# The order of VectorE's work within a step: a group's results behind the norm, a joining group's sums behind the statistics

## The chip, the cores and the metric

The kernel runs on one core of a Trainium2 chip. The time is the device time of one launch in microseconds (us). Before the change the median of three runs is 4190.81 us (4182.11 to 4192.11).

The core has engines with an instruction queue each, which work side by side and wait for one another through semaphores: TensorE (PE in the profile; its weight loads are PEld) for matmuls and transposes, VectorE (DVE), ScalarE (ACT), GpSimd (POOL), and SyncE (SP), which issues DMAs. TensorE writes its results into PSUM, a small memory that VectorE and ScalarE read; everything else lies in SBUF.

## What is computed

12,500 nodes with 256 channels each go through one graph layer and then, each node for itself, through 30 iterations of a small network. All is fp32.

```python
xn = layernorm(x)
x = x + relu(segment_sum((xn @ W_gnn)[src] * edge_weight, dst)) + mix(xn)   # 200,000 edges

def step(h):                       # 30 times
    h = h + 0.01 * tanh(h)
    h = h * sigmoid(h)
    h = layernorm(h) * ln_w + ln_b
    return h @ W + b

x = x + step applied 30 times to layernorm(x)
```

`mix` is a linear attention over all nodes; what is left of it per node, once its key-value products are summed, is one 256 x 256 matrix. The gains and offsets of the layernorm are folded into the matrices beforehand.

## The kernel before

**Tiles and groups.** The nodes lie in 98 tiles of 128 rows, and four tiles make a group: 24 groups of 1024 columns per partition and one of 512. A first part (the first 470 us or so) normalises x, sums the key-value products and prepares the matrices. The rest, which the change is about, is a loop over 803 steps.

**Items and steps.** A planner, `plan`, gives each step `k` at most one item: `("mix", g)`, the product of group g with the matrix of mix; `("W", g)`, the product of its gathered and summed neighbours with the graph weight; or `("pass", g, it)`, one of the 30 iterations. There are 25, 23 and 750 of them. Up to five groups are between their first and last pass at the same time (`ABREAST`), and a group's passes are at least four steps apart (`APART`). The planner has its own costs in us for an item, a gather and so on; they decide only which item stands in which step. The instructions of each engine stand in the order in which the loop writes them: nothing is reordered later.

**An item takes three steps.** Its work is spread so that TensorE always has something that is ready:

- step k: for a pass, the transposes of the normalised group `z` into PSUM (`transposes`, line 1057), copied by ScalarE to `zT` (line 1064);
- step k + 1: the product, `matrix` (line 1070), sixteen matmul passes into the PSUM tile `po`. There are two `po` buffers, so the product of step k + 1 writes the buffer that the product of step k - 1 wrote and that step k reads;
- step k + 2: what is done with the product. For a pass, ScalarE's tanh (`act1`, line 1016), VectorE's sum h + 0.01 tanh(h) (`act2`, line 1022), which is the last reader of `po`, and ScalarE's SiLU (line 1023). After that `stats`: VectorE's statistics (`bn_stats`, line 1029), and GpSimd's variance plus epsilon (line 1033) and power -1/2 (`rs`, line 1035). For the last pass of a group, VectorE adds the product to `base`, the group's result (line 1129, two halves), and SP writes it out. For a mix item VectorE adds product and x (line 1135, and two more, line 1140, for the first two groups). For a W item it adds the product and the stored rows (line 1144) and then the ReLU of that to `base` (line 1145).

**The norm.** `normed` (line 1043) makes `z` from the statistics, four VectorE instructions for a full group. In step k it is called for the items of steps k + 1 and k + 2 whose statistics are there. A group whose passes are four steps apart has statistics in step k + 2, norm in k + 3 and transposes in k + 4.

**A joining group.** When a group leaves, the next one starts (`fresh`, with the step k3 in which it does). Its first layernorm and first tanh, sum and SiLU aren't a pass: statistics of `base` in k3 and k3 + 1 (lines 1195 to 1203), its normalised half in k3 + 2 and k3 + 3 (ScalarE line 1174, VectorE line 1178), its tanh at the end of k3 + 3 (line 1183, through `act1`), its sums and SiLU (`act2`, lines 1022 and 1023) in k3 + 4, its statistics at the end of k3 + 5. Its first pass can stand in k3 + 7 at the earliest. An output stands two steps after a group's last pass, which is k3 + 2 of the group that joins in its place.

**The order within a step, before.** VectorE's queue in step k has: the edge selections (lines 213 to 226), a clearing of PSUM (line 276), then the sum of the pass of step k - 2, or the output, mix or W work in its place; the joining group's sum, where k is k3 + 4; the norm; the joining group's normalised half; the statistics of the pass of step k - 2; the joining group's statistics.

Beside all this, GpSimd gathers the rows of the edges (line 187), and TensorE sums them in pieces in between (lines 239 and 261), up to about 3470 us.

Of the kernel before, what the change touches and what calls it, by code (L numbers as in the profile page):

```python
# [31 lines left out]
def gps_layer(  # L32
# [48 lines left out]
    def rows_io(ap, tl, t0, nt, load, eng):  # L81
        full = nt if (t0 + nt) * P <= N else nt - 1
        parts = []
        if full:
            parts.append((tl[:, :full, :], ap[t0 * P : (t0 + full) * P, :].rearrange("(g p) c -> p g c", p=P)))
        if full < nt:
            parts.append((tl[:TAIL, full, :], ap[(t0 + full) * P : N, :]))
        for s, d in parts:
            if load:
                eng.dma_start(out=s, in_=d)  # L90
            else:
                eng.dma_start(out=d, in_=s)
# [192 lines left out]
    class KeyValue:  # L285
# [19 lines left out]
        def normed(self):  # L305
            rs8 = kvw.tile([P, 2 * HEADS], F32, name="rs8")
            nc.vector.reciprocal(rs8, self.sd)
            nc.vector.tensor_tensor(
                kns[self.t % 3][:, :, :D], self.pkv, rs8[:, :, None].to_broadcast([P, 2 * HEADS, D]), ALU.mult
            )  # L310
# [315 lines left out]
    with tc.If(n_out > 0):  # L626
        with ExitStack() as pg_:
# [12 lines left out]
            for t in range(NE):  # L640
# [8 lines left out]
                d = gp.tile([P, 1], F32, name="d")  # L649
                nc.vector.tensor_copy(d[:rows], d_i[:rows])  # L650
                d = d[:rows]
# [354 lines left out]
    norm, zs, zTs, pos, xts, first_norm = {}, {}, {}, {}, {}, {}  # L1006
# [3 lines left out]
    def flat(h, nt):  # L1010
        return h[:, : nt // 2].rearrange("p q c j -> p (q c j)")
# [7 lines left out]
    def act2(gi, h, s):  # L1019
        nt = groups[gi][1]  # L1020
        sf = flat(s, nt)
        nc.vector.scalar_tensor_tensor(sf, sf, 0.01, flat(h, nt), op0=ALU.mult, op1=ALU.add)  # L1022
        nc.scalar.activation(sf, sf, AF.Silu)  # L1023

    def stats(gi, s):
        t0, nt = groups[gi]
        st = hp.tile([P, G // 2, 6], F32, name="st")
        for q in range(nt // 2):
            nc.vector.bn_stats(st[:, q, :], s[:, q].rearrange("p c j -> p (c j)"))  # L1029

        sv = st.rearrange("p q (j f) -> p (q j) f", f=3)
        ve = fp.tile([P, G], F32, name="ve")
        nc.gpsimd.tensor_scalar(ve[:, :nt], sv[:, :nt, 2], 1.0 / C, EPS, ALU.mult, ALU.add)  # L1033
        rs = hp.tile([P, G], F32, name="rs")
        nc.gpsimd.tensor_tensor(rs[:, :nt], ve[:, :nt], mhalf[:, :nt], ALU.pow)  # L1035
        norm[gi] = (s, sv, rs)
# [41 lines left out]
    item = lambda k: steps[k][0] if 0 <= k < K and steps[k][0] else (None, None)  # L1078
    quads_of = lambda k: steps[k][1] if k < K else 0
    fresh = []  # L1080
    written = {}
    selections(ed.summed + quads_of(0) - ed.selected)
    for k in range(K + 3):
# [33 lines left out]
        last = kind2 == "pass" and item(k - 2)[2] == FFN_ITERS - 1  # L1117
# [3 lines left out]
            copies(gi)  # L1121
        if kind2 == "pass" and not last:
            act2(g2, pos.pop((kind2, g2)), s2)
        elif last:
            t0, nt = groups[g2]
            for q in range(nt // 2):
                h = pos[kind2, g2][:, q].rearrange("p c j -> p j c")
                r = slice(2 * q, 2 * q + 2)
                nc.vector.tensor_tensor(base[g2][:, r, :], h, base[g2][:, r, :], ALU.add)  # L1129
            pos.pop((kind2, g2))  # L1130
            rows_io(out, base[g2], t0, nt, False, nc.sync)
            written[g2] = k
        elif kind2 == "mix":
            nt = groups[g2][1]
            nc.vector.tensor_tensor(base[g2], pos.pop((kind2, g2))[:, :nt, :], xts.pop((kind2, g2))[:, :nt, :], ALU.add)
            if g2 < ed.weighted:
                aT = ed.aT.pop(g2).rearrange("p k (g n) -> p k g n", n=P)
                for i in range(KC):
                    bk = base[g2][:, :, i * P : (i + 1) * P]
                    nc.vector.scalar_tensor_tensor(bk, aT[:, i], 0.0, bk, op0=ALU.max, op1=ALU.add)  # L1140
        elif kind2 == "W":
            nt = groups[g2][1]
            ac = xts.pop((kind2, g2))[:, :nt, :]
            nc.vector.tensor_tensor(ac, pos.pop((kind2, g2))[:, :nt, :], ac, ALU.add)
            nc.vector.scalar_tensor_tensor(base[g2], ac, 0.0, base[g2], op0=ALU.max, op1=ALU.add)

        for g3, k3 in fresh:
            if k == k3 + 4:  # L1150
                act2(g3, *first_norm[g3])
        for d in (1, 2):
            kind3, g3 = item(k + d)[:2]
            if kind3 == "pass" and g3 in norm:
                normed(g3)
        for g3, k3 in fresh:
            nt = groups[g3][1]
            if k in (k3 + 2, k3 + 3):
# [24 lines left out]
                    first_norm[g3] = (h, act1(g3, h))  # L1183
        if kind2 == "pass" and not last:
            stats(g2, s2)
        start = steps[k][2] if k < K else None
        if start is not None:
            fresh.append((start, k))
# [50 lines left out]
```

## Time and profile before

| | |
|---|---|
| median of 3 runs | 4190.81 us (4182.11 to 4192.11) |
| the profiled execution's own time | 4187.49 us |
| its span, first to last instruction | 4185.7 us |
| mean granted TensorE clock | 0.991 |
| VectorE busy | 3401.4 us (81%) |
| ScalarE busy | 2523.0 us (60%) |
| GpSimd busy | 2577.9 us (62%) |

One execution was profiled. The page of the profile gives the busy time of each engine, the chain of work that ended last (followed back from the last instruction, at each step to what released it), and the groups of instructions by source line with their counts and mean durations. Other views of the same trace give the waits (who waited for whom, how long in total, how often and the longest), and the timeline (start, duration, engine, line, operation, tiles written and read, shapes, count; in brackets the idle time of the engine just before, and what ended it). A tile name such as `po<-w,zT` says that `po` is written and `w` and `zT` are read. `x4` is a run of four instructions of a kind, merged.

Durations in the steps, from the groups with shapes kept apart: one sum of a pass (line 1022, 128 x 1024) 1.21 us, one norm instruction (line 1043, 128 x 256) 0.42 us, of which a full group has four that overlap a little, one statistics instruction (line 1029, 128 x 512) 0.68 us, two to a group; one half of an output (line 1129, 128 x 512) 0.68 us, the sum of a mix item (line 1135) 1.21 us, the two of a W item (lines 1144 and 1145) 1.22 and 1.23 us; ScalarE's SiLU (line 1023) 1.06 us.

### The profile page before, as it was taken

The numbers are of one execution on the slowest core, as the hardware profiler recorded it, in microseconds if no ns is written. First come the engines' busy times: TensorE is split into PE (matmuls) and PEld (weight loads), VectorE is DVE, ScalarE is ACT, GpSimd is POOL, SyncE is SP. The second block draws the span as 40 slices with busy tenths as digits, with TensorE's granted clock in tenths as the row PEclk, the third lists the DMA queues.
The fourth block names the chain that finished last, engine by engine and source line by source line (L and its number), as shares of the span: only waits on it lengthen the run. The fifth ranks groups of instructions, "written<-read, shape, count | busy, mean of one in ns | idle before, by whom it ended". The sixth has DMA issues, their size and how long they took to land.

```text
span 4185.7 us, 67249 instructions
## 1 busy us (share of the span) xinstructions
PE 4057.6 (97%) x23817; PEld 3358.3 (80%) x23817; DVE 3401.4 (81%) x7400; ACT 2523.0 (60%) x3762; POOL 2577.9 (62%) x3189
## 2 busy tenths in 40 slices
PE   8897899999999999999999999999999999999999
PEld 5444678888888888888888888888888888888888
DVE  8554568888888888888888888888888888888887
ACT  7331246666666666666666666666656666667775
POOL 3564666777777777777777777777667652222222
PEclk9898999999999999999999999999999999999999
DMA  8332532222222222222222222222222210000000
GB/s 262 108 87 72 147 98 66 65 61 65 75 61 72 76 64 74 73 66 71 72 65 72 77 65 72 70 74 61 72 70 59 65 50 14 6 6 1 1 1 23
DMA packets 147685, 278.31 MB, mean 66 GB/s; under 512 B 28048, under 2 KB 97198, under 8 KB 147342
## 3 DMA queue, kind: packets, MB, share of 16 engines
q0 software_dynamic: 75024, 204.97, 17.0%
q1 hardware_dynamic: 72173, 68.42, 5.4%
q8 instruction: 194, 3.18, 0.3%
q14 instruction: 150, 1.22, 0.1%
q10 hardware_dynamic: 144, 0.52, 0.0%
HBM read 247.68 MB, written 26.12 MB: 65 GB/s over the span
## 4 chain that ended last, share of the span: by engine, by line
PE 77%; DVE 11%; ACT 3%; issue 3%; POOL 2%; another core or an unknown queue 1%; POOLq 0%; DVEq 0%; ACTq 0%
PE po L1070 53%; PE pt L1057 13%; PE pq L239 4%; DVE z L1043 4%; PE pkv L290 3%; PE pa L261 3%; DVE st L1029 2%; DVE s L1022 2%; ACT s L1016 2%; POOL rs L1035 1%; PE pacc L316 1%; ACT s L1023 1%; POOL xg L187 0%; DVE big L1129 0%
## 5 line engine op out<-in xcount | busy, mean ns | idle before, releaser
L1070 PE MATMUL po<-w,zT 128*128 128x256 f32 x11760 | 2669.8, 380 | 4.8 <-ACT zT L1064 2.3
L1070 PEld LDWEIGHTS po<-w,zT 128*128 128x128 f32 x11760 | 2178.4, 190 | 285.2 <-issue 7.8
L187 POOL DMA_INDIRECT xg<-xnd,src_i x1563 | 1597.4, 1022 | 512.9 <-issue 308.6
L1023 ACT ACTIVATE s<-s 128x1024 f32<-128x1024 f32 (+1 forms) x750 | 780.5, 1041 | 598.5 <-DVE s L1022 584.9
L1043 DVE TENSOR_SCALAR z<-s,st,rs 128x256 f32<-128x256 f32 x2940 | 1031.5, 418 | 100.7 <-POOL rs L1035 96.0
L1029 DVE BATCH_NORM_STATS2 st<-s 128x6 f32<-128x512 f32 x1470 | 938.7, 680 | 181.6 <-ACT s L1023 163.8
L1022 DVE SCALAR_TENSOR_TENSOR s<-s,po 128x1024 f32<-128x1024 f32 x725 | 864.3, 1192 | 251.4 <-ACT s L1016 181.3
L1016 ACT ACTIVATE s<-po 128x1024 f32<-128x1024 f32 x725 | 729.6, 1006 | 209.0 <-PE po L1070 197.6
L1064 ACT ACTIVATE zT<-pt 128x512 f32<-128x512 f32 x1470 | 801.5, 602 | 61.2 <-PE pt L1057 55.0
L1057 PE MATMUL pt<-ident,z 128*128 128x128 f32 x5880 | 792.7, 276 | 38.9 <-DVE z L1043 37.5
L1057 PEld LDWEIGHTS pt<-ident,z 128*128 128x128 f32 x5880 | 670.1, 141 | 182.6 <-issue 81.6
L1035 POOL TENSOR_TENSOR rs<-ve,mhalf 128x4 f32<-128x4 f32 (+1 forms) x750 | 763.3, 1018 | 62.5
L1033 POOL TENSOR_SCALAR ve<-st 128x4 f32<-128x4 f32 (+1 forms) x750 | 147.3, 196 | 933.6 <-DVE st L1029 889.0
L250 ACT COPY sq<-pq 128x256 f32<-128x256 f32 x196 | 72.4, 369 | 284.3 <-PE pq L239 198.2
L239 PE MATMUL pq<-xg,sel 128*32 128x256 f32 x3126 | 222.9, 386 | 8.5 <-issue 6.4
L290 PE MATMUL pkv<-wkv,big 128*128 128x512 f32 x392 | 201.3, 634 | 9.3 <-DVEq L626 4.9
L239 PEld LDWEIGHTS pq<-xg,sel 128*32 128x32 f32 x3126 | 84.7, 109 | 112.1 <-issue 69.5
L261 PE MATMUL pa<-selq,sq 128*128 128x192 f32 (+1 forms) x784 | 163.4, 331 | 9.3 <-ACT sq L250 3.6
L275 ACT COPY aT<-pa 128x128 f32<-128x128 f32 x196 | 51.4, 262 | 194.1 <-PE pa L261 145.6
L261 PEld LDWEIGHTS pa<-selq,sq 128*128 128x128 f32 (+1 forms) x784 | 137.9, 192 | 22.0 <-ACT sq L250 4.7
L301 DVE TENSOR_REDUCE v<-sq 128x8 f32<-128x512 f32 x98 | 66.7, 680 | 92.4 <-ACT sq L297 78.4
L297 ACT ACTIVATE sq<-pkv 128x512 f32<-128x512 f32 x98 | 57.9, 591 | 115.3 <-PE pkv L290 69.1
(163 smaller groups left out, 1553.2 us busy)
## 6 DMA issues: line engine op xcount, KB each, us to landing
xg<-xnd,src_i POOLq DMA_INDIRECT x1563
xt<-in_x_dram SPq DMA_DIRECT2D x48, 512.0 KB
xnd<-xt SPq DMA_DIRECT2D x24, 512.0 KB
out_dram<-big SPq DMA_DIRECT2D x24, 512.0 KB
xt<-accw SPq DMA_DIRECT2D x22, 512.0 KB
ac<-accw SPq DMA_DIRECT2D x2, 512.0 KB
xg<-in_dst_dram SPq DMA_DIRECT2D x6, 128.0 KB
xg<-in_src_dram SPq DMA_DIRECT2D x6, 128.0 KB
```

The lines of the kernel that those rows point to most:

```text
L187: nc.gpsimd.indirect_dma_start(out=ed.xg[t], out_offset=None, in_=xnd, in_offset=bass.IndirectOffsetOnAxis(ap=src_i[:, t : t + 1], axis=0),)
L239: nc.tensor.matmul(ed.pq[j * 2 * WIN : (j + 1) * 2 * WIN, :], lhsT=sel[:, j, :], rhs=ed.xg.pop(q * Q + j), start=(q % 2 == 0), stop=last, ...
L261: nc.tensor.matmul(pa[:, k, :], lhsT=sq[:rows, k * P : (k + 1) * P], rhs=selq[:rows, :], start=False, stop=(o == NO - 1), skip_group_check ...
L1016: nc.scalar.activation(flat(s, nt), flat(h, nt), AF.Tanh)
L1022: nc.vector.scalar_tensor_tensor(sf, sf, 0.01, flat(h, nt), op0=ALU.mult, op1=ALU.add)
L1023: nc.scalar.activation(sf, sf, AF.Silu)
L1029: nc.vector.bn_stats(st[:, q, :], s[:, q].rearrange("p c j -> p (c j)"))
L1035: nc.gpsimd.tensor_tensor(rs[:, :nt], ve[:, :nt], mhalf[:, :nt], ALU.pow)
L1043: nc.vector.tensor_scalar(z[:, j, :], s[:, j // 2, :, j % 2], sv[:, j, 1:2], rs[:, j : j + 1], ALU.subtract, ALU.mult)
L1057: nc.tensor.transpose(pt[:, i, k, :], z[:, 2 * q + i, k * P : (k + 1) * P], ident)
L1064: nc.scalar.activation(zT[:, 2 * q : 2 * q + 2], pt, AF.Copy, bias=1.0)
L1070: nc.tensor.matmul(po[:, j // 2, :, j % 2] if paired else po[:, j, :], lhsT=lhsT(j, k), rhs=rhs[:, k, :], start=(k == 0 and (j % 2 == 0 or ...
```

## The change

Three pieces of the step's second half change places; no instruction is added or taken away. `act2` of a pass keeps its place. The norm comes directly behind it; then the outputs, mix and W work (an `elif` becomes an `if`, as the norm now stands between); then, as before, the joining group's normalised half and the statistics of the pass; and behind these the joining group's sum and SiLU, which stood ahead of the norm.

```diff
             copies(gi)
         if kind2 == "pass" and not last:
             act2(g2, pos.pop((kind2, g2)), s2)
-        elif last:
+
+
+
+        for d in (1, 2):
+            kind3, g3 = item(k + d)[:2]
+            if kind3 == "pass" and g3 in norm:
+                normed(g3)
+
+        if last:
             t0, nt = groups[g2]
             for q in range(nt // 2):
                 h = pos[kind2, g2][:, q].rearrange("p c j -> p j c")
...
             nc.vector.tensor_tensor(ac, pos.pop((kind2, g2))[:, :nt, :], ac, ALU.add)
             nc.vector.scalar_tensor_tensor(base[g2], ac, 0.0, base[g2], op0=ALU.max, op1=ALU.add)
-
-
-
-        for g3, k3 in fresh:
-            if k == k3 + 4:
-                act2(g3, *first_norm[g3])
-        for d in (1, 2):
-            kind3, g3 = item(k + d)[:2]
-            if kind3 == "pass" and g3 in norm:
-                normed(g3)
         for g3, k3 in fresh:
             nt = groups[g3][1]
             if k in (k3 + 2, k3 + 3):
...
         if kind2 == "pass" and not last:
             stats(g2, s2)
+        for g3, k3 in fresh:
+            if k == k3 + 4:
+                act2(g3, *first_norm[g3])
         start = steps[k][2] if k < K else None
         if start is not None:
             fresh.append((start, k))
```

## The prediction

> **What bounds the kernel now.** I read the page first. The chain that ended last is three quarters TensorE, and TensorE's engine row is busy for 97% of the span.
>
> ```profile
> PE 4057.6 (97%) x23817; PEld 3358.3 (80%) x23817; DVE 3401.4 (81%) x7400; ACT 2523.0 (60%) x3762; POOL 2577.9 (62%) x3189
> ...
> PE 77%; DVE 11%; ACT 3%; issue 3%; POOL 2%; another core or an unknown queue 1%; POOLq 0%; DVEq 0%; ACTq 0%
> ```
>
> So a step costs what TensorE needs for it: eight transposes 0.87 us and sixteen matmul passes 3.46 us, start to start, with now and then the edge sums between. Whatever the other engines do is free until TensorE waits for it, and what it waits for is in the table of its waits from 470 us on, where the scheduled steps run (total us, times, longest):
>
> ```profile
> PE pt L1057 <- DVE z L1043: 37.5, 41, 2.4
> PE po L1070 <- DVE s L1022: 2.5, 5, 1.5
> ...
> PE po L1070 <- DVE xt L1144: 1.1, 2, 0.5
> PE po L1070 <- DVE big L1135: 0.5, 2, 0.3
> PE po L1070 <- DVE big L1129: 0.3, 1, 0.3
> ```
>
> The first row is what an earlier norm can win, 37.5 us at the very most. The other rows matter as much: PSUM holds two step results (`po`), so the product of step k+1 overwrites the result that VectorE reads in step k. The last three rows are that wait for exactly the instructions now moved back; today it is rare.
>
> **First part: outputs, mix and W behind the norm.** Nothing is added or removed. In each of 56 steps a block (outputs 2 x 0.68 us, line 1129; mix 1.21, line 1135; W 1.22 + 1.23, lines 1144 and 1145) changes places with the norm, four instructions of 1.38 us together, 1.28 until what follows them starts. A step with W, in the timeline (start, length):
>
> ```profile
> 2951.77 1.22 DVE L1144 TENSOR_TENSOR xt<-po,xt 128x1024 f32<-128x1024 f32 x1
> 2953.02 1.23 DVE L1145 SCALAR_TENSOR_TENSOR big<-xt,big 128x1024 f32<-128x1024 f32 x1
> 2954.16 1.38 DVE L1043 TENSOR_SCALAR z<-s,st,rs 128x256 f32<-128x256 f32 x4
> ...
> 2952.64 1.04 PE L1057 MATMUL pt<-ident,z 128*128 128x128 f32 x8
> 2953.51 2.76 PE L1070 MATMUL po<-w,zT 128*128 128x256 f32 x12
> ```
>
> Today W's sum lets go of `po` at 2952.99 and the product starts at 2953.51, in time by 0.52. With the norm first (its `rs` is long there) the sum runs 2953.05 to 2954.27: TensorE waits 0.8. And what does the earlier norm win? The transposes that read it start at 2958.06, 3.9 us after its present start. Nothing. I read all 56 steps so: norm at the later of VectorE free and `rs` ready, then the sum, against the start of the next product. Late are 10 of 13 mixes (14.1 us), 12 of 22 W (11.2) and 11 of 21 outputs (14.1), 39.4 in all. Where `rs` isn't ready, VectorE now idles for it, which the sum used to cover; this makes the worst ones (2.1 to 2.6). Waits of 1.6 on products and of 3.0 on transposes stand in the same steps today and are in the 39.4: **+35**. Bounds: 0, if VectorE's queue stands emptier than I read, to +39. I take the reading, since the rows give the release to 0.05 us. The output's DMA from SP leaves 1 to 3 us later and is no one's wait except at the very end, where no norm stands before it.
>
> **Second part: the joining group's sums behind the statistics.** Its line 1022 (1.22 us) moves behind the norm (1.28) and the statistics (1.2), about 2.5 us later. ScalarE's order stays, so its SiLU of the joining group (1.06) comes 2.5 us later too, and queued behind it on ScalarE are the next step's tanh, its copies of zT and its SiLU. A join as it is:
>
> ```profile
> 3502.25 1.22 DVE L1022 SCALAR_TENSOR_TENSOR s<-s,po 128x1024 f32<-128x1024 f32 x1 [1.23 <-ACT s L1016]
> 3503.39 1.22 DVE L1022 SCALAR_TENSOR_TENSOR s<-s,big 128x1024 f32<-128x1024 f32 x1
> 3503.51 2.19 ACT L1023 ACTIVATE s<-s 128x1024 f32<-128x1024 f32 x2 [0.31 <-DVE s L1022]
> 3504.52 1.37 DVE L1043 TENSOR_SCALAR z<-s,st,rs 128x256 f32<-128x256 f32 x4
> 3505.08 1.31 PE L1057 MATMUL pt<-ident,z 128*128 128x128 f32 x8 [1.70 <-DVE z L1043]
> ...
> 3505.61 1.00 ACT L1016 ACTIVATE s<-po 128x1024 f32<-128x1024 f32 x1
> ...
> 3505.82 1.28 DVE L1029 BATCH_NORM_STATS2 st<-s 128x6 f32<-128x512 f32 x2
> ...
> 3507.01 1.20 DVE L1022 SCALAR_TENSOR_TENSOR s<-s,po 128x1024 f32<-128x1024 f32 x1
> ...
> 3508.50 1.38 DVE L1043 TENSOR_SCALAR z<-s,st,rs 128x256 f32<-128x256 f32 x4 [0.29 <-POOL rs L1035]
> ...
> 3509.68 1.04 PE L1057 MATMUL pt<-ident,z 128*128 128x128 f32 x8
> ```
>
> The gain: the norm starts at 3503.39, the transposes 0.56 behind it at 3503.95, and of the wait of 1.70 there go 1.13. The price: statistics 3504.69 to 3505.97, joining sums until 3507.10, its SiLU 3507.14 to 3508.20. The tanh, at 3505.61 today, starts at 3508.20 and ends at 3509.2. VectorE's next sums come at 3509.26, 2.25 late; the norm after them at 3510.40 rather than 3508.50; its transposes at 3510.96. TensorE would have been there at 3503.95 + 4.60 = 3508.55, so it waits 2.4, and stands 1.3 behind today's 3509.68. The joining group's own statistics and power on POOL, the last before its first pass, move by 1.9, and its first transposes from 3514.42 to 3516.3: 1.9 lost in this join.
>
> Carried on so through 23 joins (the first two have no other passes beside them): the waits of today that go are 11.8 us; 12 joins lose 1.6 to 1.9 net (21.6), 7 about 0.5 (3.5), four nothing, where a W or mix step leaves ScalarE free: **+25** net. Bounds: -12, if ScalarE's later start is caught up before a transpose, to +29, if no slack at POOL takes 0.29 off. I take +25, since in these steps VectorE's rows stand end to start and four groups in turn leave each norm only one step ahead.
>
> **What they share.** In 11 joins a late output holds TensorE for about 1.0 two steps before, while ScalarE's and VectorE's chain in the join hangs on the joining group's norm and tanh, not on TensorE. So the same us is not lost twice: -11. The mixes before 660 us meet waits on the norm that stand there already, 3 more: **-14** (bounds -25 and 0).
>
> **The clock.** In the steps there are two half-speed stretches of 3.4 us in the granted clock, at 2690 and at 3564, each just after TensorE waited 2.35 for a joining step's norm; sixteen passes then take 5.28 where 3.62 is usual, 1.7 lost. A third wait of 2.36 passed free, and so did one of 1.79. These two go (-3.4), and about two of the new waits of over 2 us should pay it again: 0, bounds -3.4 and +10 (six more).
> The Trainium skill (TensorE: Matmul & The Clock Gate, "HAM oscillation") has idle gaps above about 3.4 us as what throttles the array. By it no wait here, old or new, would cost clock, and these two stretches would not be there; the rows say otherwise, and I go by them.
>
> **Sum.** 35 + 25 - 14 + 0 = +46 us. On the profiled execution that is 4185.7 + 46 = 4231.7 of span, 4233.5 with the 1.8 around it; the median of the runs shown lies 3.3 above that execution: **4237 us**.
>
> **Rivals.** (1) *Only the results are late*: the joins come out even, ScalarE (60% busy) making good its 2.5 us; nothing is shared then except early on, and half of the lateness is absorbed by steps in which VectorE runs ahead: 35/2 to 35 - 3, 4208 to 4222. For: ScalarE waits 562 us for line 1022's sums in the steps. Against: just in the join it does not. (2) *The clock multiplies*: each of some 12 new waits near 2 us costs a half-speed stretch, 12 x 1.7 = 20, and one feeds the next: about 4262. For: 2 of 3 today. Against: waits of 1.7 to 1.8 went free. (3) *No difference*: all lands in slack, 4191. Against: TensorE has about 50 us of idle in 3,700 us of steps. (4) *Faster*: the norm is the one late thing in a joining step. With it ahead of the sums the 11.8 us go, also the 3.0 beside outputs and W, and 3.4 of clock, 18 in all: 4173. It decides if the wait for `po` and ScalarE's queue together cost under 18 us, a third of a us for each moved block. For: the 37.5 us are the largest wait there is. Against: the W step above, where the norm had 3.9 us to spare.
>
> **How the numbers follow.** Forecast 4237, own range 4222 to 4262, chance 0.60; rival 1 0.20; rival 2 0.08; rival 3 0.06; rival 4 0.06. The range 4205 to 4262 takes in the forecast's and rival 1's. What a measurement of this kernel can tell from no change is about 0.3%, 12.6 us: slower than 4203.4 is 0.88 (all of the first three but a little of rival 1), within 0.07, faster 0.05.
>
> **What would show it.** Right: TensorE's waits for lines 1129, 1135 and 1144 (by their new numbers) grow from 2 to some 30 us; waits on the norm fall in the joining step and rise in the two steps after; ScalarE waits over 2 us for the joining sums. Wrong: if the waits for `po` stay under 10 us, my release times are off; if the norm's wait falls well below 37.5 in total, the chain through ScalarE is off, and rival 4 is near.

## The result, and the profile after

The changed kernel takes 4240.94 us (median of four runs, 4235.25 to 4242.6) against 4187.83 us of the kernel before (median of four, the three shown above and one more, 4182.11 to 4192.11): 53.1 us more, a ratio of 1.0123 with a 95% interval of 1.0109 to 1.0137. The forecast was 4237, 46 us above the kernel before, with a range of 4222 to 4262.

The page of the changed kernel, engine rows and the chain that ended last:

```profile
PE 4066.9 (96%) x23817; PEld 3361.1 (79%) x23817; DVE 3404.7 (80%) x7400; ACT 2520.3 (59%) x3762; POOL 2599.7 (61%) x3189
...
PE 69%; DVE 16%; ACT 4%; issue 4%; POOL 3%; another core or an unknown queue 1%; DMA 0%; DVEq 0%; POOLq 0%; ACTq 0%
```

VectorE's busy time is what it was (3401.4 before), as nothing was added. But on the chain TensorE has 8% of the span less than before (69% for 77%), and VectorE has 5% more, ScalarE and GpSimd 1% each: TensorE now stands and waits. For whom, its waits in the steps tell (total us, times, longest); outputs, mix and W are lines 1137, 1143 and 1152 here:

```profile
PE pt L1057 <- DVE z L1043: 44.5, 42, 3.6
PE po L1070 <- DVE big L1137: 11.8, 10, 2.1
PE po L1070 <- DVE xt L1152: 9.7, 9, 1.9
PE po L1070 <- DVE big L1143: 9.2, 6, 2.0
PE po L1070 <- DVE s L1022: 4.1, 6, 1.5
```

The three rows for results that let go of `po` late come to 30.7 us in 25 waits, where they were 1.9 in five. The wait on the norm, which the change puts first, isn't less than before but more, 44.5 for 37.5. Half-speed stretches of 3.4 us are seven among the passes instead of two.

The W step that the prediction showed, now (start, length; in brackets the idle time before and what ended it):

```profile
2984.51 1.37 DVE L1043 TENSOR_SCALAR z<-s,st,rs 128x256 f32<-128x256 f32 x4
2985.37 1.04 PE L1057 MATMUL pt<-ident,z 128*128 128x128 f32 x8
2985.81 1.21 DVE L1152 TENSOR_TENSOR xt<-po,xt 128x1024 f32<-128x1024 f32 x1
2987.05 1.22 DVE L1153 SCALAR_TENSOR_TENSOR big<-xt,big 128x1024 f32<-128x1024 f32 x1
...
2987.07 3.29 PE L1070 MATMUL po<-w,zT 128*128 128x256 f32 x14 [0.67 <-DVE xt L1152]
```

From the transposes to the product it is 1.70 us rather than 0.87, so 0.83 are lost; 0.8 was worked out. The product starts 0.05 behind the end of W's sum, and the norm that W's sum had to let past is for transposes that start at 2991.73.

And the join that the prediction carried through, from the joining step on:

```profile
3549.80 1.38 DVE L1043 TENSOR_SCALAR z<-s,st,rs 128x256 f32<-128x256 f32 x4
...
3550.36 1.32 PE L1057 MATMUL pt<-ident,z 128*128 128x128 f32 x8
3551.10 1.28 DVE L1029 BATCH_NORM_STATS2 st<-s 128x6 f32<-128x512 f32 x2
...
3552.30 1.21 DVE L1022 SCALAR_TENSOR_TENSOR s<-s,big 128x1024 f32<-128x1024 f32 x1
...
3553.54 1.06 ACT L1023 ACTIVATE s<-s 128x1024 f32<-128x1024 f32 x1 [2.56 <-DVE s L1022]
3554.50 1.01 ACT L1016 ACTIVATE s<-po 128x1024 f32<-128x1024 f32 x1
...
3555.54 1.22 DVE L1022 SCALAR_TENSOR_TENSOR s<-s,po 128x1024 f32<-128x1024 f32 x1 [2.04 <-ACT s L1016]
3556.68 1.38 DVE L1043 TENSOR_SCALAR z<-s,st,rs 128x256 f32<-128x256 f32 x4
...
3557.23 1.32 PE L1057 MATMUL pt<-ident,z 128*128 128x128 f32 x8 [2.10 <-DVE z L1043]
```

The wait of 1.70 in front of the first transposes is gone. ScalarE, though, stands 2.56 us before the joining group's SiLU, the tanh of the next pass comes behind that, VectorE stands 2.04 us for the tanh, and TensorE 2.10 us for the norm one step later, where it didn't wait at all before.

### The profile page after: what moved, and what is told of

Its sections match the earlier page's. It is cut to its first block, busy times and chain, and to the rows that moved or that the text cites. A ratio compares the mean times of both kernels' runs of the same rounds, so it can differ in the third digit from the quotient of the medians.

```text
span 4240.8 us, 67172 instructions
## 1 busy us (share of the span) xinstructions
PE 4066.9 (96%) x23817; PEld 3361.1 (79%) x23817; DVE 3404.7 (80%) x7400; ACT 2520.3 (59%) x3762; POOL 2599.7 (61%) x3189
## 4 chain that ended last, share of the span: by engine, by line
PE 69%; DVE 16%; ACT 4%; issue 4%; POOL 3%; another core or an unknown queue 1%; DMA 0%; DVEq 0%; POOLq 0%; ACTq 0%
PE po L1070 48%; PE pt L1057 12%; DVE z L1043 6%; PE pq L239 4%; DVE st L1029 4%; DVE s L1022 3%; PE pa L261 2%; PE pkv L290 2%; ACT s L1016 2%; POOL rs L1035 2%; ACT s L1023 1%; PE pacc L316 1%; POOL xg L187 1%; DVE big L1137 0%
## 5 line engine op out<-in xcount | busy, mean ns | idle before, releaser
L1070 PE MATMUL po<-w,zT 128*128 128x256 f32 x11760 | 2678.7, 381 | 35.9 <-DVE big L1137 11.8
L1057 PE MATMUL pt<-ident,z 128*128 128x128 f32 x5880 | 794.7, 276 | 47.1 <-DVE z L1043 44.5
L1033 POOL TENSOR_SCALAR ve<-st 128x4 f32<-128x4 f32 (+1 forms) x750 | 168.0, 224 | 976.4 <-DVE st L1029 932.6
```

Of the source, the lines that this page charges most:

```text
L1057: nc.tensor.transpose(pt[:, i, k, :], z[:, 2 * q + i, k * P : (k + 1) * P], ident)
L1070: nc.tensor.matmul(po[:, j // 2, :, j % 2] if paired else po[:, j, :], lhsT=lhsT(j, k), rhs=rhs[:, k, :], start=(k == 0 and (j % 2 == 0 or ...
```

## The experiments

Each ratio is against the kernel before on the same chip. The chip that ran the first four took 4087.58 us for the kernel before, 100 us less than the others did; some 80 of these lie ahead of the first pass (its transposes begin at 391 us in `e1_results` and at 474 in the profile of the kernel before). So times of whole kernels are compared on the same chip only. The kernel before has one profile, from one of the slower chips; where a stretch of it is set beside one of the first four, the text says so. `e4_silu_late` is one of these four and takes nearly the time of the kernel before, so the others are set beside it too.

**One part alone.** `e1_results` leaves the joining sums where they stood and moves only the results behind the norm:

```diff
+        for g3, k3 in fresh:
+            if k == k3 + 4:
+                act2(g3, *first_norm[g3])
         for d in (1, 2):
...
             stats(g2, s2)
-        for g3, k3 in fresh:
-            if k == k3 + 4:
-                act2(g3, *first_norm[g3])
```

(a diff against the changed kernel, with lines left out at `...`). 

> Outputs, mix and W work behind the norm; the joining group's sums ahead of the norm as in the kernel before. Theory (PSUM is let go of late): TensorE's waits for the three lines that read po come to 28 to 32 us as in the changed kernel, waits on the norm stay at 34 to 38, two to four half-speed stretches in the steps: 4188 + 28 to 36 = 4216 to 4224 us. Rival (only the joining group's part costs): waits for po of a few us at most, 4183 to 4193.

Measured: 4115.31 for 4087.58, +27.7 us, ratio 1.0070 (1.0056 to 1.0084). TensorE's waits in the steps (outputs, mix and W are lines 1140, 1146 and 1155):

```profile
PE pt L1057 <- DVE z L1043: 18.1, 26, 1.8
PE po L1070 <- DVE big L1140: 11.5, 10, 2.1
PE po L1070 <- DVE big L1146: 11.3, 10, 2.0
PE po L1070 <- DVE xt L1155: 9.6, 9, 2.8
```

The waits for `po` are all there, 32.4 us, so this loss needs nothing of the other part. The time all but fits (28 to 36 expected), but the wait on the norm does not: 18.1 rather than 34 to 38. A late output holds TensorE back by 1 to 2 us just ahead of the joining step, whose norm then comes in time. So this part also takes some of the old waits off. Behind step 148, where the mix steps are nearly over, it needs 14.3 us more than the kernel before (3038.0 for 3023.7, each in its one profile, on two chips). From the first transposes of a pass to step 148 it needs 9.4 us more than `e4_silu_late` on the same chip (676.3 for 666.9).

`e2_joining` moves only the joining sums behind the statistics. 

> Only the joining group's sums moved behind the statistics; the results ahead of the norm as in the kernel before. Theory (ScalarE's queue stands behind the late SiLU): waits for po as in the kernel before, waits on the norm 55 to 65 us rather than 37.5 (12 gone in the joining steps, 35 new in the two steps behind them), 4188 + 20 to 29 = 4208 to 4217. Rival (it wins what the joining step's norm waited): 4170 to 4180.

Measured: 4121.31, +33.7 us, ratio 1.0086 (1.0072 to 1.0099); it was dearer than expected. Its waits:

```profile
PE pt L1057 <- DVE z L1043: 48.6, 44, 2.5
PE po L1070 <- DVE s L1022: 3.6, 7, 1.5
```

The waits on the norm are 48.6, less than the 55 to 65 expected, and half-speed stretches are four instead of two. From step 148 to the last pass this kernel needs 3046.0 us and the kernel before 3023.7 (each in its one profile, on two chips): 22.3 more there, of which 12.8 are waits on the norm (39.5 for 26.7) and 1.7 the one extra stretch that lies there (three for two).

**Is it VectorE's order or ScalarE's queue?** `e3_join_mid` puts the joining sums between norm and statistics, 1.3 us late rather than 2.5. 

> The joining group's sums between norm and statistics: 1.3 us later than in the kernel before, where the change has 2.5. Theory (ScalarE's queue): the tanh behind its SiLU comes some 1.0 to 1.3 late, which about balances the norm's 1.13 in the joining step: 4182 to 4194, no difference that counts. Rival (any place behind the norm costs, as VectorE's order alone does it): 4208 to 4217 as with the joining part alone.

Measured: 4092.19, +4.6 us, ratio 1.0013 (1.0004 to 1.0022). The place behind the norm alone hardly costs. `e4_silu_late` keeps VectorE's order of `e2_joining` to the instruction and moves one instruction of ScalarE (a diff against `e2_joining`, with lines left out at `...`):

```diff
-    def act2(gi, h, s):
+    def act2(gi, h, s, silu=True):
...
-        nc.scalar.activation(sf, sf, AF.Silu)
+        if silu:
+            nc.scalar.activation(sf, sf, AF.Silu)
...
+        for g3, k3 in fresh:
+            if k == k3 + 5:
+                sf = flat(first_norm[g3][1], groups[g3][1])
+                nc.scalar.activation(sf, sf, AF.Silu)
         for d in (1, 2):
...
             if k == k3 + 4:
-                act2(g3, *first_norm[g3])
+                act2(g3, *first_norm[g3], silu=False)
```

> The joining group's sums behind the statistics, as in the change, and its SiLU on ScalarE one step later, behind the next pass's tanh, copies and SiLU; results ahead of the norm. VectorE's order is that of the joining part alone. Theory (what costs is the tanh queued behind the late SiLU on ScalarE): the loss goes and the gain at the norm stays, 0.3 to 1.0 us per join and the clock: 4173 to 4183. Rival (VectorE's late sums themselves cost, through the joining group's statistics): 4205 to 4217.

Measured: 4084.70, 2.9 us less than the kernel before, ratio 0.9993 (0.9984 to 1.0002): 36.6 us better than `e2_joining`, and by itself no difference that can be told (5 to 15 us below it were expected). Its waits on the norm, and the same join in its timeline from the joining step's norm on (norm, transposes and product stand one line further down):

```profile
PE pt L1058 <- DVE z L1044: 24.5, 29, 1.8
```

```profile
3401.19 1.38 DVE L1044 TENSOR_SCALAR z<-s,st,rs 128x256 f32<-128x256 f32 x4
...
3402.27 1.01 ACT L1016 ACTIVATE s<-po 128x1024 f32<-128x1024 f32 x1
...
3403.68 1.21 DVE L1022 SCALAR_TENSOR_TENSOR s<-s,big 128x1024 f32<-128x1024 f32 x1
...
3404.81 1.22 DVE L1022 SCALAR_TENSOR_TENSOR s<-s,po 128x1024 f32<-128x1024 f32 x1
...
3406.07 1.39 DVE L1044 TENSOR_SCALAR z<-s,st,rs 128x256 f32<-128x256 f32 x4
...
3406.63 1.32 PE L1058 MATMUL pt<-ident,z 128*128 128x128 f32 x8
```

The tanh comes 1.08 behind the norm's start, where it was 4.70 in the change. VectorE goes from the joining group's sums to the next pass's without a gap, and the transposes of that next pass don't wait. Over the whole run the waits on the norm are 24.1 us shorter than in `e2_joining` (24.5 for 48.6), and no half-speed stretch is left among the passes where there were four, worth some 1.7 us each: together about 31 of the 36.6. What the joining part costs is ScalarE's queue behind a SiLU whose input comes late; VectorE's order costs nothing that can be told.

**Is it PSUM or VectorE's idling?** In the results part VectorE also idles for `rs` before the norm, which the results used to cover. `e6_results_copy` keeps that order and lets ScalarE take the product out of PSUM at once, from step 146 on, into the place of a group that is written (a diff against `e1_results`, with lines left out at `...`):

```diff
+        if kind2 and (last or kind2 != "pass") and 1 in written and written[1] + 2 <= k:
+            nt = groups[g2][1]
+            po, cp = pos.pop((kind2, g2)), base[1].rearrange("p g c -> p (g c)")
...
+                nc.scalar.copy(cp[:, :nt, :], po[:, :nt, :])
+            pos[kind2, g2] = cp
         if kind == "pass":
             copies(gi)
```

> Results behind the norm as in the results part alone, but from step 146 on ScalarE first copies the product from PSUM to SBUF (one copy of 1.0 us in 44 steps) and VectorE adds from there. VectorE's order stays that of the results part. Theory (the loss is PSUM let go of late): of that part's 32 us of waits for po the 24 behind step 146 go, the 8 before it stay: 2 to 9 us above the kernel before on the same chip. Rival (VectorE itself loses time, as it now idles for rs before the norm): 22 to 32 above, as with the results part alone.

Measured: 4199.18 for 4187.61, +11.6 us, ratio 1.0027 (1.0015 to 1.0039). Its waits (outputs, mix and W are lines 1150, 1156 and 1165):

```profile
PE pt L1057 <- DVE z L1043: 33.2, 31, 2.9
...
PE po L1070 <- DVE big L1156: 2.8, 4, 1.7
PE po L1070 <- DVE xt L1165: 2.5, 3, 1.2
...
PE po L1070 <- DVE big L1150: 1.6, 1, 1.6
```

All of these 6.9 us for `po` lie before step 148, where nothing is copied; behind it there is none, where `e1_results` has 24.5. So the wait is the late release of PSUM. The norm has its waits back too (27.0 behind step 148, 13.2 in `e1_results`, 26.7 before). The time is a little above the expected 2 to 9; behind step 148 this run lost 5.6 us against the kernel before, with four half-speed stretches there instead of two (each in its one profile, on two chips).

`e7_w_split` moves just the second instruction of a W item, which doesn't read `po`, behind the norm of the kernel before. 

> The kernel before with only the second instruction of a W item (the ReLU into base, 1.23 us, which doesn't read po) behind the norm, 23 times. Theory: no wait for po comes up, and the norm of a W step has us to spare, so -2 to +1 us against the kernel before on the same chip. Rival (anything moved behind the norm in a W step costs, as VectorE's queue is full there): +5 to +12.

Measured: 4186.60, ratio 0.9999 (0.9986 to 1.0012): no cost. It is the read of `po` that must not come late, not a W item's work.

**The parts together.** `e5_change_again` is the changed kernel on another chip. 

> The changed kernel itself, beside the single parts. The parts alone cost 27.7 (results) and 33.7 us (joining sums). Theory (both hold TensorE, and where a late output stands two steps before a joining step the same us is not lost twice): 8 to 14 less than their sum, so 47 to 54 above the kernel before on the same chip. Rival (the parts don't meet): 58 to 65 above.

Measured: 4247.60 for 4187.61, +60.0, ratio 1.0144 (1.0129 to 1.0159), against 61.4 for the sum of the parts. The expectation (47 to 54) failed here, and the time is the rival's (58 to 65): by these medians the parts share 1.4 us, by the first comparison (53.1) 8.3, and the runs don't settle it. The waits are the same as in the first profile: 44.4 on the norm, 31.2 for `po`.

`e9_change_silu_late` is the change with ScalarE's SiLU one step later (the diff of `e4_silu_late`), `e10_change_both_mended` has the copy out of PSUM as well (that of `e6_results_copy`). The order of VectorE's instructions is the change's own in both. 

> The changed kernel with one thing mended: the joining group's SiLU one step later on ScalarE. Theory: the joining part's loss goes, the results part's stays, so waits for po of 28 to 32 us as in the change, waits on the norm 15 to 25 rather than 44, 20 to 32 us above the kernel before on the same chip. Rival (together the two parts cost through VectorE's order, whatever ScalarE does): 40 and more above.

> The changed kernel with both mended: the SiLU one step later, and from step 146 on ScalarE's copy of the product, from which VectorE adds. VectorE's order is the change's own. Theory: waits for po only in the first 146 steps (about 8 us), waits on the norm 20 to 28, 1 to 10 us above the kernel before on the same chip. Rival (as above): 25 and more above.

Measured: 4215.01 for 4188.70, +26.3 (1.0044 to 1.0069), and 4195.97, +7.3 (1.0004 to 1.0029). The joining part's loss is gone from the first, that of the results part has stayed, with 32.9 us of waits for `po` (28 to 32 expected); its outputs, mix and W are lines 1142, 1148 and 1157:

```profile
PE pt L1058 <- DVE z L1044: 19.0, 23, 1.8
PE po L1071 <- DVE big L1142: 11.8, 10, 2.1
PE po L1071 <- DVE xt L1157: 11.5, 9, 2.6
PE po L1071 <- DVE big L1148: 9.6, 7, 2.0
```

The second, with outputs, mix and W in lines 1152, 1158 and 1167:

```profile
PE pt L1058 <- DVE z L1044: 28.6, 30, 2.9
...
PE po L1071 <- DVE big L1158: 2.6, 3, 1.7
PE po L1071 <- DVE xt L1167: 2.6, 3, 1.2
...
PE po L1071 <- DVE big L1152: 1.6, 1, 1.6
```

That is 28.6 on the norm and 6.8 for the results in `po`. Of the change's 53 to 60 us all but some 7 are gone while VectorE's order is unchanged.

**A faster version.** `e8_both` has what was free: joining sums behind the statistics with their SiLU one step later, and W's second instruction behind the norm. 

> The joining sums behind the statistics with their SiLU one step later on ScalarE, and the W item's ReLU behind the norm. Theory: what the late SiLU alone won (2.9) and at most 2 more: 1 to 6 us below the kernel before on the same chip. Rival (the two meet in VectorE's queue): at or above it.

Measured: 4180.48 for 4187.61, 7.1 us less where 1 to 6 were expected, ratio 0.9985 (0.9977 to 0.9994). It is below the kernel before by more than its interval, though by little.

## Why the prediction was right, point by point

- *The results release PSUM late*: right, and shown by `e1_results` and `e6_results_copy`. The size was 37.8 us of new waits for `po` (39.4 less the 1.6 there) and came out at 28.8 (30.7 less 1.9). Outputs came to 11.8 in 10 waits (14.1 in 11 read), W to 9.7 in 9 (11.2 in 12), mixes to 9.2 in 6 (14.1 in 10). The reading of 56 steps took each product's start as it stood; once TensorE has been held in one step, the next ones are due later. That this is the whole difference isn't shown.
- *The earlier norm wins nothing in these steps*: right for the W step shown. But the late outputs take waits on the norm away one joining step later, 13.5 us of them behind step 148 in `e1_results`. That is what the prediction called shared.
- *ScalarE's queue*: right, shown by `e4_silu_late` and again by `e9_change_silu_late`. The chain of the join shown went as worked out: transposes in time, 2.1 us of wait one step later (2.4 predicted). From the step ahead of the joining step to two steps behind it, TensorE's delay against the kernel before grew by 1.3 us (46.9 to 48.2), where 1.9 was worked out, as the late output ahead of it had already taken the rest of the old wait.
- *+25 for the joins and -14 shared*: by these terms the waits on the norm were to become 37.5 - 11.8 - 3.0 + 37 - 14 = 45.7 (37 being the net 25 and the 11.8 that go), and are 44.5. The terms don't hold one by one: the joining part alone cost 33.7 us where 25 stood, the results part alone 27.7 where 35 stood, and the parts together cost 1 to 8 less than apart where 14 stood. These misses have opposite signs, so that the sum came near is in part luck. The sharing is with waits that were there before, inside the results part, and not so much between the parts.
- *The clock at 0*: mis-sized. Seven half-speed stretches among the passes instead of two make 5 x 1.7 = 8.5 us; the bounds were -3.4 to +10. I had counted on the two old ones going and about two new waits that pay; the two went, and seven new ones came. The rule on idle gaps that the prediction set against the row (the Trainium skill, TensorE: Matmul & The Clock Gate, "HAM oscillation") would have one of the seven at most, behind the one wait of 3.6; the others came with waits of 1.4 to 2.3 us.
- *The sum*: 46 forecast, 53.1 measured. From the first transposes of a pass to the last ones the profiles differ by 57.8 us. Waits for `po` +28.8, on the norm +7.0 and the clock +8.5 make 44.3 of them, and other waits of TensorE some 5. Another 4 lie between a group's transposes and the product behind them, in gaps of under 0.15 us, which the table of waits leaves out; the last 4 to 5 I could not place.
- *Rivals*: that ScalarE would make good its 2.5 us fell with `e2_joining`. That the norm is the one late thing in a joining step is half true: with its SiLU out of the way (`e4_silu_late`) the wait on it falls to 24.5, but that is worth 3 us, not 18. The clock didn't multiply: five stretches more, not twelve. ScalarE's wait for the sums of line 1022, given there as 562 us, is 583.6 in the table from 470 us on; nothing rests on it.

## What to carry to other kernels

Before work is moved back in an in-order queue, look up what it lets go of: here a read of a double-buffered PSUM tile was due within 0.5 us, while the work put ahead of it had 3.9 us to spare. Then follow the moved instruction's result into the next engine's queue: its consumer stands in program order there too, and holds everything behind it. For the joining sums only the order on that second engine was wrong, and moving the consumer by one step mended it at no cost that could be told (-2.9 us, `e4_silu_late`).

## What the runs showed of the hardware

The half-speed clock can come after shorter waits than the 2 us that the prediction counted on. Over the passes of the twelve profiles (the wait ahead of the last transposes left out, as nearly nothing comes behind it), of 135 idle stretches of TensorE between 1.2 and 1.75 us four had a half-speed stretch begin at them or within 3.5 us, of 16 between 1.75 and 2.0 five, of 31 between 2.0 and 2.5 twenty-two, and of six above 2.5 all six. In the changed kernel, for one:

```profile
3601.90 5.11 PE L1070 MATMUL po<-w,zT 128*128 128x256 f32 x16 [2.05 <-DVE big L1137]
3606.84 1.04 PE L1057 MATMUL pt<-ident,z 128*128 128x128 f32 x8
3607.72 3.62 PE L1070 MATMUL po<-w,zT 128*128 128x256 f32 x16
```

Behind a wait of 2.05 us for an output the sixteen passes take 5.11 us, with the granted clock at a half from 3601.33 to 3604.74; the next sixteen are back at 3.62. So in these profiles a wait of 2 to 2.5 us cost nearly twice itself in about two cases of three. What decides between the cases, the runs don't show.
